# Two outlook-attention layers on one core: when the zeros of layer 0's weight tables are written

## The chip, the cores and the metric

The kernel runs on one core of a Trainium2 chip. TensorE (PE) multiplies matrices; VectorE (DVE), ScalarE (ACT) and GpSimd (POOL) work on elements; SyncE (SP) does no arithmetic here and issues most of the transfers (DMAs), each engine in its own program order. All transfers share 16 DMA engines. The metric is the device time of the whole program in microseconds, the median of several runs.

## The reference

Two layers follow each other on an image batch `x` of 8 × 56 × 56 × 384 numbers (float32), each as `x = x + layer(groupnorm(x))`. In layer 0 every pixel makes, for 12 heads, a 9 × 9 softmax from its own channels and uses it to mix the values of its 3 × 3 neighbourhood; the nine results are added back at the nine neighbours:

```
v    = einsum('bhwc,oc->bhwo', x, Wv);  vp = pad(v)
attn = softmax((x @ Wa.T).reshape(b, n, heads, 9, 9) * d ** -0.5, axis=-1)
out  = einsum('bnhpq,bnqhd->bnphd', attn, patches(vp))
y    = sum over p of out[:, :, :, p], shifted to neighbour p
return y @ Wo.T
```

Layer 1 is the same idea with 6 heads, 9 weights a pixel and no adding back. Before each layer the mean and variance of 32 groups of channels are taken per image.

## The kernel before

**Tiling.** Two images make a pair: `IMG * H` = 112 lines on the partitions. Four pairs follow each other, and within a pair the 56 columns of the image are the steps of layer 0's main loop, so a step is one column of 112 pixels. Of every eight columns seven are computed; the eighth rides in the 16 spare partitions of the seven.

**A step.** `attend` makes three score products (`bank<-wa_t`) and one value product (`bank<-wv_t`) on PE; DVE takes the maximum and subtracts it, ACT takes the exponential. Between the products other work is put in a fixed order: `stats_chunk` transposes a third of a block of the next pair's input (`pt<-xr`, four matmuls) for its group norm and keeps it in HBM (`xT`), `normalise` divides the softmax of the column before, `presum` and `fold` (four columns behind) add up the weights that meet in one pixel, and `keep_v` writes the values to a table `vtab0` in HBM through a tile `v` of two buffers.

**The weight tables.** `fold` leaves a column's weights in one of four buffers `wts` and SP writes them to a table in HBM (`ztab<-wts`, two DMAs for each patch the column belongs to). There are two tables in layer 0, `ztab0[0]` and `ztab0[1]`; patches of seven columns use them in turn. A table has 112 lines of 41 KB between margins of two and three lines. Of each of the 11 slots in a line only five of eleven rows are written by `fold`; the rest, and the margins, must be zero. The first column of the second table is written in step 9. From step 12 on `fetch_z` reads a patch of a table back (`z<-ztab`), and `contract` multiplies it by the values (`pc<-z,vp`).

**The zeros.** `fill` (line 215) writes zeros from one tile to any place of a table by one DMA on SP. `clear_weights` fills one table by seven of them: two margins, the head of each line (110 KB), two fills between the slots (1213 KB each) and two single rows. The second of the fills between reaches over the end of a line into the head of the next, so its issue waits until the fill of the heads has landed. Table 0 is filled by `clear_first` before the first step, behind the keeping of pair 0's transposed input, the zeros of `vtab0` and two fills for the first two slots of table 0. Table 1 is filled in step 3, from a list `clears` that `upkeep` works off at the end of each step.

**What sets the order.** Every engine's order is the program's (`keep_in_program_order`). In `upkeep`, the list of clears comes ahead of `stats_load`, the load of the next block of the next pair (`xr<-in_x`, 672 KB). The load that `upkeep` issues in step 3 is first used by the transposes of step 6. Transfers put into `later` (the `last` rows, residuals, results) go out at the end of a step, after `upkeep`. Every DMA of SP also waits until an earlier one with the same completion semaphore has landed; there are eight of these, taken in turn.

Of the kernel before, what the change touches and what calls it, by code (L numbers as in the profile page):

```python
# [15 lines left out]
def two_outlook_layers(  # L16
# [38 lines left out]
    R = IMG * H  # L55
    MARGIN = 2
# [16 lines left out]
    E0 = 2 * K - 1  # L73
# [8 lines left out]
    PY0, NPY0, SX0, SY0 = 7, 8, PX + 4, 11  # L82
    ROW0 = HEADS0 * PX
# [9 lines left out]
    EP0, FIRST0 = 11, 3  # L93
    EP1, FIRST1 = 11, 4
    SLOT0, SLOT1 = EP0 * ROW0, EP1 * ROW1
    LINE0, LINE1 = SX0 * SLOT0 + ROW0, SX1 * SLOT1 + ROW1
# [22 lines left out]
    ztab0 = [dram.tile([RT + 1, LINE0], F32, name=f"ztab0_{n}") for n in range(NTAB0)]  # L119
# [89 lines left out]
    def fill(table, first, dims, width):  # L209

        src = zeros[: dims[0][1], :width]
        if len(dims) > 1:
            src = src.unsqueeze(1).to_broadcast([dims[0][1], dims[1][1], width])
        tc.keep_in_program_order(
            nc.sync.dma_start(bass.AP(table.tensor, table.offset + first, [*dims, [1, width]]), src)
        )

    def clear_v(table, sx, pad):

        line = sx * C  # L220
        part = line // 12
        fill(table, 0, [[(R + GAP) * line, NPX + 1], [part, 12 * GAP]], part)
        fill(table, GAP * line, [[line, R], [C, pad]], C)
        fill(
            table, ((NPX - 1) * (R + GAP) + GAP) * line + (sx - pad) * C,
            [[line, R], [C, pad]], C,
        )

    def clear_weights(table, line, part, sx, slot, row, first, e, ep):
        fill(table, 0, [[part, MARGIN * line // part]], part)  # L230
        fill(table, (MARGIN + R) * line, [[part, (MARGIN + 1) * line // part]], part)
        top = MARGIN * line
        fill(table, top, [[line, R]], first * row)
        for n in range(2):
            between = top + (first + e) * row + n * (ep - e) * row // 2
            fill(table, between, [[line, R], [slot, sx]], (ep - e) * row // 2)

        fill(table, top + first * row, [[slot, sx]], row)
        fill(table, top + (R - 1) * line + (first + e - 1) * row, [[slot, sx]], row)

    def clear_first():

        clear_v(vtab0, SX0, 2)
        for n in range(2):
            first = MARGIN * LINE0 + FIRST0 * ROW0 + n * SLOT0
            fill(ztab0[0], first, [[LINE0, R], [E0 * ROW0 // 2, 2]], E0 * ROW0 // 2)
        clear_weights(ztab0[0], LINE0, 366, SX0, SLOT0, ROW0, FIRST0, E0, EP0)

    def clears():

        yield 3, lambda: clear_weights(
            ztab0[1], LINE0, 366, SX0, SLOT0, ROW0, FIRST0, E0, EP0
        )
        yield (NPAIR - 1) * W + 4, lambda: clear_v(vtab1, SX1, 1)
        for n, t in enumerate(ztab1):
            yield (NPAIR - 1) * W + 10 + 8 * n, lambda t=t: clear_weights(
                t, LINE1, 350, SX1, SLOT1, ROW1, FIRST1, K, EP1
            )
# [12 lines left out]
    def sort_columns(t, by, i, engine):  # L271
        engine(
            t[:, i].rearrange("k (j p) -> k j p", j=NCH), by[:, i].rearrange("k (p j) -> k j p", j=NCH)
        )

    def norm_params(st, name, params, key):

        mv = stat.tile([P, IMG, 2], F32, tag="mv", name=f"mv_{name}")

        def over_groups(src, what):  # L280
            pg = ps.tile([P, IMG], F32, tag="t", name=f"p{what}_{name}")
            matmul(pg, gmat, src, start=True, stop=True)
            g = stat.tile([P, IMG], F32, tag=what, name=f"{what}_{name}")
            vector.tensor_copy(g, pg)
            return g

        for b in range(IMG):
            vector.bn_aggr(mv[:, b, :], st[:, b].rearrange("p i n s -> p (i n) s"))
        yield
        mean = over_groups(mv[:, :, 0], "gmean")  # L290

        part = stat.tile([P, IMG], F32, tag="part", name=f"part_{name}")
        vector.tensor_sub(part, mv[:, :, 0], mean)
        vector.tensor_mul(part, part, part)
        vector.tensor_add(part, part, mv[:, :, 1])
        yield
        var = over_groups(part, "gvar")
        std = stat.tile([P, IMG], F32, tag="std", name=f"std_{name}")
        scalar.activation(std, var, AF.Sqrt, bias=eps_t)
        scale = const.tile([P, IMG], F32, name=f"scale_{name}")  # L300
        vector.reciprocal(scale, std)
        bias = const.tile([P, IMG], F32, name=f"bias_{name}")
        vector.scalar_tensor_tensor(bias, mean, -1.0, scale, ALU.mult, ALU.mult)
        params[key] = scale, bias
        yield
# [120 lines left out]
    def layer0(late, pools):  # L426
# [12 lines left out]
        def stats_load(pair, blk, queue, xr):  # L439
            xrs[pair, blk] = xr  # L440
            queue.dma_start(xr, xf[pair * R : (pair + 1) * R, blk * XB : (blk + 1) * XB, :])
# [3 lines left out]
        def xr_tile(pair, blk):  # L445
            t = xr_bufs[blk % 2]
            return t[:R].rearrange("r (m c) -> r m c", m=XB)
# [130 lines left out]
        def load(g):  # L578
            pair, blk = divmod(g, NBLK)
            xins[g] = io.tile([P, XB, NCH, R], F32, tag="xin", name=f"xin_{g}", bufs=1)  # L580
            sync.dma_start(
                xins[g], xTs[pair][:, blk * XB : (blk + 1) * XB]
            )

        def normed(g, parts, both=False):

            scale, bias = params[g // NBLK]
            xin, to = xins[g], xns[g // 2 % 2]
            n = XB - g % 2
            for shared, b in parts:  # L590
                rows = slice(b * H, (b + 1) * H)
                if shared:
                    if not g % 2:
                        continue
                    dst = to[:, :, :, R + b * PART : R + (b + 1) * PART]
                    src = xin[:, n, :, rows].rearrange("p i (j y) -> p i j y", j=NTILE)
                else:
                    dst = to[:, :, g % 2 * XB : g % 2 * XB + n, rows]
                    src = xin[:, :n, :, rows].rearrange("p m i r -> p i m r")
                if both and b:  # L600
                    vector.tensor_scalar(
                        dst, src, scale[:, b : b + 1], bias[:, b : b + 1], ALU.mult, ALU.add
                    )
                else:
                    scalar.activation(
                        dst, src, AF.Identity, bias=bias[:, b : b + 1], scale=scale[:, b : b + 1]
                    )
# [275 lines left out]

        making = {}
        clearing = list(clears())

        def upkeep(step):

            pair, c = divmod(step, W)
            if pair == 0:  # L890
                if c == 1:
                    gpsimd.memset(wts, 0.0)
                if c == 3:
                    by = z_flat[0][:, : NCH * C].rearrange("p (i n) -> p i n", i=NCH)
                    sync.dma_start(by, wo0.rearrange("(i p) n -> p i n", p=P))
                if 5 <= c < 5 + NCH:
                    by = z_flat[0][:, : NCH * C].rearrange("p (i n) -> p i n", i=NCH)
                    sort_columns(wo_t, by, c - 5, vector.tensor_copy)
            while clearing and clearing[0][0] <= step:
                clearing.pop(0)[1]()  # L900
            if pair + 1 < NPAIR:
                blk, i = divmod(c - 3, NCH)
                if i == 0 and blk < NBLK - 1 and pair + c:
                    stats_load(pair + 1, blk + 1, sync, xr_tile(pair + 1, blk + 1))
                if NBLK * NCH + 3 <= c < NBLK * NCH + 6:
                    if c == NBLK * NCH + 3:
                        making["0"] = norm_params(stats.pop(pair + 1), f"0_{pair + 1}", params, pair + 1)
                    next(making["0"])
            g, j = divmod(step + 2 * XB, XB)
            if j < NCH and g < NPAIR * NBLK:  # L910
                normed(g, SHARED if j == IMG else WHOLE[j : j + 1])
            if step < IMG:
                normed(1, WHOLE[step : step + 1])
            if j == NCH - 1 and 2 < g + 1 < NPAIR * NBLK and g > 2:
                load(g + 1)
# [413 lines left out]
```

## Time and profile before

| what | value |
|---|---|
| time, median of 3 runs | 3188.24 us (3183.09 to 3190.77) |
| the profiled execution: its time | 3187.7 us |
| its span | 3185.5 us |
| mean granted TensorE clock | 0.989 |
| busy: PE, DVE, POOL, ACT | 96%, 65%, 52%, 32% |
| DMA queue of SP and ACT (q1) | 711.31 MB, 73.7% of 16 engines |
| DMA queue of POOL (q0) | 116.90 MB, 11.8% |
| zeros of tables 0 and 1 | 14 DMAs, issued between 70.5 and 103.8 us |

The profile is of one execution, in microseconds from its first instruction. A row of the timeline gives start, length, engine, line, operation, what it writes and reads, how many were merged, and in brackets how long the engine was idle before it and what ended that. "SPq" rows are DMA issues of SP: their length is the time the issue held the queue, and the transfer lands later. Until about 57 us the kernel takes the statistics of pair 0; then step 0 begins, and a step takes 6 to 9 us. Columns are numbered like the steps; on PE a column's end is its value product `bank<-wv_t`.

### The profile page before, as it was taken

The page shows a single profiled execution, that of the slowest core. Times are in us where ns is not written, and L with a number is a line of the kernel's source. Part 1 is how long each engine was busy: PE and PEld are TensorE (multiplying, and loading weights), DVE is VectorE, ACT ScalarE, POOL GpSimd, SP SyncE. Part 2 cuts the span into 40 slices and gives each one's busy share as a digit, 9 for nine tenths or more (in the row PEclk, how much of TensorE's full clock was granted, in tenths as well). Part 3 has the DMA queues.
Part 4 walks back from the last instruction along what each step waited for, and adds up shares of the span by engine and source line. Part 5 has one row for each costly group of instructions (what it writes and reads, how often), then busy time and mean ns, then how long its engine had stood idle before and what let it go on. Part 6 is the DMA issues. An engine that isn't in the chain of part 4 may idle for free. (4 is left out here: it accounts for less than half of the span.)

```text
span 3185.5 us, 72855 instructions
## 1 busy us (share of the span) xinstructions
PE 3065.3 (96%) x27640; PEld 2093.4 (66%) x27640; DVE 2084.8 (65%) x4942; ACT 1005.2 (32%) x2422; POOL 1654.2 (52%) x2759
## 2 busy tenths in 40 slices
PE   6899999999999999999999999989999999999997
PEld 5667766777776677776776666645666565656655
DVE  5777777777777777777777777635454555555454
ACT  4333333343333334333333333222222222222221
POOL 2765665655556565656566566544334344434431
PEclk8999999999999999999999999999999999999999
DMA  9799987899997899988888987889899988989897
GB/s 303 225 306 319 307 273 260 300 296 300 325 311 235 275 305 303 314 280 286 280 250 262 309 275 247 286 279 242 219 230 246 234 235 228 251 222 241 233 236 154
DMA packets 619842, 850.86 MB, mean 267 GB/s; under 512 B 264926, under 2 KB 496562, under 8 KB 611170
## 3 DMA queue, kind: packets, MB, share of 16 engines
q1 hardware_dynamic: 522322, 711.31, 73.7%
q0 software_dynamic: 63824, 116.90, 11.8%
q10 hardware_dynamic: 33344, 17.98, 2.1%
q8 instruction: 218, 3.57, 0.5%
q14 instruction: 134, 1.10, 0.1%
HBM read 514.86 MB, written 322.17 MB: 263 GB/s over the span
## 5 line engine op out<-in xcount | busy, mean ns | idle before, releaser
L128 PE MATMUL bank<-wa_t,xn 128*128 128x288 f32 x3528 | 967.8, 411 | 15.7 <-ACT xn L143 10.3
L128 PE MATMUL po<-yT,wo_t 128*128 128x448 f32 (+1 forms) x2304 | 817.0, 497 | 26.5 <-DVE x1t L143 19.4
L143 POOL TENSOR_TENSOR at<-at,d 128x972 f32<-128x972 f32 x196 | 441.2, 2251 | 714.8 <-DVE d L143 387.7
L128 PEld LDWEIGHTS bank<-wa_t,xn 128*128 128x128 f32 x3528 | 647.7, 191 | 226.2 <-issue 17.6
L128 PEld LDWEIGHTS po<-yT,wo_t 128*128 128x128 f32 x2304 | 433.6, 191 | 328.7 <-issue 195.8
L143 ACT ACTIVATE at<-at 128x972 f32<-128x972 f32 (+1 forms) x228 | 215.3, 944 | 997.1 <-DVE at L143 992.3
L1104 POOL DMA_DIRECT2D at<-lgt x392 | 204.8, 526 | 591.9 <-DVE lgt L143 580.8
L143 DVE TENSOR_REDUCE mx<-bank 128x36 f32<-128x324 f32 x588 | 284.8, 484 | 311.2 <-PE bank L128 309.3
L128 PE MATMUL bank<-wc_t,xn 128*128 128x438 f32 x1176 | 478.8, 543 | 5.1 <-DMA wc_t<-in_wv 5.1
L143 ACT COPY yT<-pc 128x294 f32<-128x294 f32 (+2 forms) x512 | 198.5, 405 | 804.9 <-PE pc L128 803.5
L128 PE MATMUL bank<-wv_t,xn 128*128 128x384 f32 x1176 | 414.5, 489 | 0.0
L128 PEld LDWEIGHTS pc<-z,vp 121*32 121x32 f32 (+1 forms) x17664 | 337.6, 120 | 111.9 <-issue 69.2
L128 PE MATMUL pc<-z,vp 121*32 121x49 f32 (+1 forms) x17664 | 374.2, 218 | 23.2 <-DMA z<-ztab 7.9
L128 PEld LDWEIGHTS bank<-wc_t,xn 128*128 128x128 f32 x1176 | 215.6, 191 | 180.9 <-issue 167.8
L143 DVE TENSOR_TENSOR at<-bank,mx 128x324 f32<-128x324 f32 x588 | 291.5, 496 | 31.0
L128 PEld LDWEIGHTS bank<-wv_t,xn 128*128 128x128 f32 x1176 | 220.8, 190 | 132.0 <-issue 9.3
L143 POOL DMA_DIRECT2D vtab<-v x476 | 289.5, 612 | 12.2 <-issue 6.8
L143 POOL TENSOR_TENSOR pre<-at,at 112x108 f32<-112x108 f32 (+1 forms) x440 | 236.5, 538 | 85.0 <-DMA at<-at 36.2
L143 DVE TENSOR_TENSOR lgt<-bank,ba_t 128x54 f32<-128x54 f32 x196 | 42.0, 214 | 308.7 <-PE bank L128 308.7
L333 POOL DMA_DIRECT2D vtab<-v x392 | 211.6, 544 | 16.0 <-issue 7.8
L143 DVE SCALAR_TENSOR_TENSOR wide<-po,bo_t,wide 128x448 f32<-128x448 f32 (+1 forms) x156 | 97.5, 625 | 167.4 <-PE po L128 167.3
L143 ACT ACTIVATE wts<-pre,inside 112x48 f32<-112x48 f32 (+4 forms) x672 | 179.3, 358 | 78.1 <-DMA ztab<-wts 66.2
(111 smaller groups left out, 2816.9 us busy)
## 6 DMA issues: line engine op xcount, KB each, us to landing
z<-ztab SPq DMA_DIRECT2D x64, 2352.0 KB
vp<-vtab SPq DMA_DIRECT2D x64, 1536.0 KB
vp<-vtab SPq DMA_DIRECT2D x64, 945.0 KB
xres<-xT SPq DMA_DIRECT2D x32, 1176.0 KB
ztab<-wts SPq DMA_DIRECT2D x336, 110.2 KB
vtab<-v POOLq DMA_DIRECT2D x108, 336.0 KB, 6.6
xin<-xT SPq DMA_DIRECT2D x52, 672.0 KB
xr<-in_x SPq DMA_DIRECT2D x50, 672.0 KB
```

Of the source, the lines that this page charges most:

```text
L128: tc.keep_in_program_order(nc.tensor.matmul(*args, **kwargs))
L143: return lambda *args, **kwargs: tc.keep_in_program_order(op(*args, **kwargs))
L333: queue.dma_start(bass.AP(table.tensor, table.offset + first, [*([line * step, count] for step, count in rows_of or ((1, rows),)), *([[(R ...
L1104: nc.gpsimd.dma_start(at_of(g_of)[row : row + n, m_of].rearrange("r k h -> r (k h)"), lg[lo : lo + n])
```

## The change

`clear_weights` is divided into `clear_lines`, which fills a range of lines (heads and the two fills between the slots), and `clear_rest` (margins and the two single rows). For layer 0's tables the lines are filled in four pieces of 28, one at the end of a step: table 0 in steps 1 to 4 and its rest in step 5, table 1 in steps 7 to 10 and its rest in step 11. `clear_first` keeps the zeros of `vtab0` and the two fills of the first slots. The work on the list moves behind `stats_load` in `upkeep`. In layer 1 the tables are still filled whole, with the rest now ahead of the lines. The bytes are the same; SP issues 32 DMAs for the two tables where it issued 14, and 1800 rows in all against 1782. The order of the instructions on PE, DVE, ACT and POOL does not change.

```diff
-    def clear_weights(table, line, part, sx, slot, row, first, e, ep):
+    def clear_lines(table, line, sx, slot, row, first, e, ep, lo, hi):
+        top = (MARGIN + lo) * line
+        fill(table, top, [[line, hi - lo]], first * row)
+        for n in range(2):
+            between = top + (first + e) * row + n * (ep - e) * row // 2
+            fill(table, between, [[line, hi - lo], [slot, sx]], (ep - e) * row // 2)
+
+    def clear_rest(table, line, part, sx, slot, row, first, e):
         fill(table, 0, [[part, MARGIN * line // part]], part)
         fill(table, (MARGIN + R) * line, [[part, (MARGIN + 1) * line // part]], part)
         top = MARGIN * line
-        fill(table, top, [[line, R]], first * row)
-        for n in range(2):
-            between = top + (first + e) * row + n * (ep - e) * row // 2
-            fill(table, between, [[line, R], [slot, sx]], (ep - e) * row // 2)
-
         fill(table, top + first * row, [[slot, sx]], row)
         fill(table, top + (R - 1) * line + (first + e - 1) * row, [[slot, sx]], row)
+
+    def clear_weights(table, line, part, sx, slot, row, first, e, ep):
+        clear_rest(table, line, part, sx, slot, row, first, e)
+        clear_lines(table, line, sx, slot, row, first, e, ep, 0, R)
...
-        clear_weights(ztab0[0], LINE0, 366, SX0, SLOT0, ROW0, FIRST0, E0, EP0)
 
     def clears():
 
-        yield 3, lambda: clear_weights(
-            ztab0[1], LINE0, 366, SX0, SLOT0, ROW0, FIRST0, E0, EP0
-        )
+        for step, table in ((1, ztab0[0]), (7, ztab0[1])):
+            for n in range(4):
+                yield step + n, lambda t=table, n=n: clear_lines(
+                    t, LINE0, SX0, SLOT0, ROW0, FIRST0, E0, EP0, n * R // 4, (n + 1) * R // 4
+                )
+            yield step + 4, lambda t=table: clear_rest(t, LINE0, 366, SX0, SLOT0, ROW0, FIRST0, E0)
...
-            while clearing and clearing[0][0] <= step:
-                clearing.pop(0)[1]()
             if pair + 1 < NPAIR:
                 blk, i = divmod(c - 3, NCH)
                 if i == 0 and blk < NBLK - 1 and pair + c:
                     stats_load(pair + 1, blk + 1, sync, xr_tile(pair + 1, blk + 1))
...
+            while clearing and clearing[0][0] <= step:
+                clearing.pop(0)[1]()
```

## The prediction, made before the changed kernel was run

> **What bounds the kernel now.** I read the page first, then a cut of the trace into stretches of about one column each, then the timelines of SP, PE and DVE where a stretch is poor, then the waits. The page's busy shares and its slices:
>
> ```profile
> PE 3065.3 (96%) x27640; PEld 2093.4 (66%) x27640; DVE 2084.8 (65%) x4942; ACT 1005.2 (32%) x2422; POOL 1654.2 (52%) x2759
> PE   6899999999999999999999999989999999999997
> PEclk8999999999999999999999999999999999999999
> ```
>
> PE bounds the run: 120.2 us of the 3185.5 us span are all that it idles, and over a third of this lies in the first 300 us. What a change near the start can win is PE's idle time there; afterwards PE is full, so a saving stays. The cut by stretches (columns: PE, PEld, DVE, ACT, POOL busy with counts, PE clock, DMA share, GB/s):
>
> ```profile
> 78.00:87.00 9.00, 7.90 (x32) 5.24 (x31) 7.18 (x17) 1.93 (x3) 8.92 (x13) 1.00 0.93 271
> 95.50:103.00 7.50, 7.50 (x35) 5.62 (x34) 5.29 (x13) 3.02 (x6) 4.68 (x9) 1.00 1.00 299
> 103.00:111.50 8.50, 1.55 (x7) 0.88 (x5) 5.91 (x12) 2.08 (x3) 6.68 (x10) 0.87 0.93 292
> 111.50:119.00 7.50, 7.47 (x25) 5.77 (x26) 3.11 (x8) 1.27 (x4) 4.97 (x11) 0.69 0.52 148
> 128.00:135.00 7.00, 7.00 (x33) 5.34 (x32) 4.77 (x11) 3.62 (x8) 4.84 (x11) 1.00 0.28 81
> 135.00:143.00 8.00, 7.63 (x34) 5.53 (x33) 7.29 (x18) 3.52 (x8) 6.18 (x10) 1.00 0.64 169
> 143.00:151.00 8.00, 7.54 (x33) 5.38 (x32) 7.29 (x20) 2.69 (x7) 6.48 (x10) 1.00 0.70 203
> 151.00:159.00 8.00, 7.86 (x35) 5.46 (x33) 7.40 (x18) 2.70 (x7) 5.48 (x9) 1.00 0.76 239
> ```
>
> One stretch stands out: from 103 to 111.5 PE works 1.55 of 8.5 us, and in the next its clock is 0.69. In 135 to 159 DVE is as full as PE (21.98 of 24 us). The timeline of PE there:
>
> ```profile
> 83.50 1.72 PE L128 MATMUL bank<-wa_t,xn 128*128 128x288 f32 x6 [1.10 <-ACT v L143]
> 92.26 1.72 PE L128 MATMUL bank<-wa_t,xn 128*128 128x288 f32 x6 [1.33 <-ACT v L143]
> 111.53 0.99 PE L131 MATMUL pt<-ident,xr 112*128 112x112 f32 x4 [6.98 <-DMA xr<-in_x]
> 112.32 3.11 PE L128 MATMUL bank<-wa_t,xn 128*128 128x288 f32 x6
> ```
>
> PE waits 6.98 us for the second input block of pair 1, and works the next product at a lower clock (3.11 us; the others take 1.72). SP's timeline says why the block is late:
>
> ```profile
> 64.56 23.14 SPq L215 DMA_DIRECT2D ztab<-zeros  x9
> 91.63 12.20 SPq L215 DMA_DIRECT2D ztab<-zeros  x7
> 104.35 1.09 SPq L143 DMA_DIRECT2D xr<-in_x  x1
> ```
>
> SP spends 35 us on the fills of the two tables; the load is issued behind both. The timeline of DVE and two answers of SP's waits (58 to 104 us, then 119 to 159) give the rows for the costs:
>
> ```profile
> 115.47 0.50 DVE L143 TENSOR_REDUCE mx<-bank 128x36 f32<-128x324 f32 x1 [6.26 <-PE bank L128]
> ```
> ```profile
> SPq L215 <- DMA ztab<-zeros: 7.8, 2, 4.6
> ```
> ```profile
> SPq L143 <- DVE wts L143: 23.8, 5, 8.9
> ```
>
> **The change, part by part.**
>
> (a) Column 6's wait goes. PE, DVE, ACT and POOL keep their order; SP alone changes. Ahead of the load now stand the two band fills (SP is through them at 70.5), the pieces of columns 1 and 2 (six fills), two writes to `last` and Wo's load. A piece's third fill overlaps its first, so SP waits until that has landed; the next piece's first waits for the third. That is three landing waits ahead of the load. The two such waits of before took 3.2 and 4.6 us (7.8 less 4.6), so 9.6 to 13.8 us. The nine issues: before, nine fills took 23.14 less 3.2, or 2.2 us each, and seven 12.20 less 4.6, or 1.1 each: 9.9 to 19.8 us. So the load goes out between 70.5 + 19.5 = 90 and 70.5 + 33.6 = 104 us, against 104.35. I take about 92: the fills are a quarter as large, and the slow issues were those behind the older writes. Landing took at most 7.2 us (104.35 to 111.53): about 99. PE is ready for the block at 104.55 (111.53 less 6.98), so the wait disappears.
>
> Its worth: PE's distance from column 5's to column 6's value product is 117.53 less 100.99, 16.5 us; the later distances are 7.2 and 7.8 (126.43, 133.60, 141.40), so by PE alone 9.0 us come back, clock included. DVE says less: its gap is 6.26 us, and behind it DVE works nearly without a break. In the 16 us from 103 to 119 it was busy 9.02; at the 0.916 of 135 to 159 that takes 9.85 us, 6.2 saved. Both ends stay; I take 6.3, as DVE is the fuller engine in the columns after.
>
> (b) The waits of 1.10 and 1.33 us in columns 3 and 4 are for `v` buffers whose writes to `vtab` land late among table 0's zeros. The first lies before the pieces can thin the traffic; the second should go. 1.3 taken, 0 to 2.4 possible.
>
> (c) Table 1's 2.74 MB of zeros (110 + 2 × 1213 + 200 + 7 KB) move from 91 to 104 us into columns 7 to 11. At the 299 GB/s of 95.5 to 103 that is 9.2 us of DMA time. Free in 128 to 159: 0.72 × 7 + 0.36 × 8 + 0.30 × 8 + 0.24 × 8 = 12.2 us. It fits, with 3 us to spare, so its cover is thin; next would come late `v` landings, as in (b). I charge one of these, 1.2; bounds 0 and 9.2.
>
> (d) SP issues 32 fills in place of 14, and the 4 pieces of table 1 each add one landing wait. Queued behind are that column's xT and `last` writes, the next column's `ztab` writes, in column 10 the load of xin, in column 11 vp's fetch. Those who wait for them are ACT and DVE for a `wts` buffer (two or more columns later), POOL for `last`, ACT for xin. SP stands free 23.8 us in five waits, 4.8 a column; a piece needs 3.2 to 4.6 plus three issues of 0.4: 4.4 to 5.8. Cost 0 taken, 4 × 1.0 the upper end. Table 0's margins, filled in column 5, wait for the weight writes just issued (one more landing, 3.2 to 4.6) and column 6's weight write for them; 0 taken, since that write is next awaited two columns on. Layer 1's fills change only their order within a table: 0.
>
> A rule speaks against (d): in the Trainium skill, DMA: Bandwidth & Descriptors, Rules for kernel authors, small transfers are to be coalesced, and Anatomy of one DMA there gives each about 2.0 us that do not shrink with size. By it 18 more would cost an estimated 36 us, were each on the path. The rows above show landing waits even longer than that, but on a queue with idle time.
>
> The same page (Why a DMA increments its semaphore by 16 and not by 1) says that a DMA uses the largest number of engines up to 16 that divides its outermost dimension, 14 for a 28-line piece. By it (c) would be an estimated 10.5 us. No row of the run before has a 28-line transfer.
>
> Sum: −6.3 − 1.3 + 1.2 = −6.4 us. The profiled execution took 3187.7 us, 0.5 below the median of the runs shown (3188.24): 3181.3 on its own time, 3181.8 on the median; I say 3181.5. From 159 us on DMA is next to bound (0.95 and more to 200 us, with fetches of `vp` and `z`); those move up with the columns and get no new bytes, the pieces being out by column 11.
>
> **Rivals.**
> - PE's reckoning holds, and both `v` waits go: 9.0 + 2.4 = 11.4, 3176.8 us. For it: the slow clock after the wait costs 1.4 us on one product alone. Against: DVE at 92% afterwards.
> - The load is no earlier: at the slow end of (a) it goes out at 104. Nothing is won: 3188. For it: fills took 2.2 us each to issue. Against: those stood behind the 9.4 MB of pair 0's transposed input, which the DMAs have written by about 70 us (376 GB/s from 65 to 72 us, 125 from 72 to 78).
> - Slower: SP becomes the bound of columns 7 to 10. Without pieces it is busy 3.2 us of 7.8 there (issues of 1.80, 0.49, 0.59 and 0.35 from 144.5 on). A landing wait above 3.4 us (7.8 − 3.2 − 1.2) begins to make it late; at 5.0 us four columns have eaten the 6.4; at 7.4 us, about what the late `xr` took to land (7.2), they cost 16 and the run ends at 3198, 0.3% above before. Against: DMA is at 0.28 to 0.76 there, `v` landing in 3.3 to 5.1 us between 128 and 150, and `wts` gives two columns of room.
>
> **How the numbers follow.** Forecast 0.42, PE's reckoning 0.30, load no earlier 0.15, slower 0.13. A measurement tells about 0.3% (9.6 us) from no change, so the forecast and the unmoved load are "same" save for the upper edge of the first, PE's reckoning "faster": 0.33, 0.53, 0.14. The range goes from PE's reckoning less half the spread of the three runs (3176.8 − 3.8 = 3173) to no gain plus the same (3188.2 + 3.8 = 3192); the slow case and a larger gain are left out.
>
> **What would show it.** After: SP issues the second `xr` near 92 us, PE's 6.98 us wait on `xr` and the clock of 0.69 are gone, column 6's value product comes about 6 to 9 us earlier, DVE has no gap over 1 us there; in columns 7 to 11 the DMA share rises to about 0.9 with no new PE wait over 1.5 us; every later landmark is earlier by the same amount. Wrong if SP waits for a fill's landing over 5 us a piece, if a new wait for `xr`, `xin` or `wts` opens before column 16, or if PE's idle time from 160 to 210 us grows.

## The result and the profile after

| | before | after |
|---|---|---|
| median of 6 runs | 3187.59 us (3183.09 to 3197.83) | 3203.02 us (3199.51 to 3206.35) |
| ratio to before, 95% interval | | 1.0044 (1.0028 to 1.0060) |
| span of the profiled execution | 3185.5 us | 3199.7 us |
| mean granted clock | 0.989 | 0.986 |

The change makes the kernel 0.44% slower, 15 us by the medians and 14.2 by the spans. The forecast was 3181.5 us, and the range ended at 3192: both missed. The page of after, its busy shares and its first rows of slices:

```profile
PE 3071.8 (96%) x27640; PEld 2097.9 (66%) x27640; DVE 2081.8 (65%) x4942; ACT 1005.8 (31%) x2422; POOL 1651.9 (52%) x2759
...
PE   6879999999999999999999999989999999999998
...
PEclk8989999999999999999999999989999999999999
```

PE did the same 27640 matmuls. Its third slice (160 to 240 us) has fallen from 9 to 7, and the clock there from 9 to 8: the loss lies early, and where it lies can be read from one landmark per column, the start of its value product `bank<-wv_t` (us, from the timelines of PE):

| column | 5 | 6 | 8 | 12 | 13 | 14 | 16 | 17 | 18 |
|---|---|---|---|---|---|---|---|---|---|
| before | 100.99 | 117.53 | 126.43 | 157.28 | 165.33 | 173.07 | 188.32 | 197.04 | 209.63 |
| after | 101.59 | 108.77 | 120.17 | 152.30 | 161.61 | 173.29 | 196.96 | 205.68 | 223.80 |
| difference | +0.6 | −8.8 | −6.3 | −5.0 | −3.7 | +0.2 | +8.6 | +8.6 | +14.2 |

Column 6's gain is there; from column 12 on it is lost, and by column 18 the whole 14.2 us of the end are made. After 230 us the two profiles stay 14 to 18 us apart. The cut of after by the stretches shown of before (PE, PEld, DVE, ACT, POOL busy with counts, clock, DMA share, GB/s), with one for columns 13 to 18 added:

```profile
95.50:103.00 7.50, 7.09 (x33) 5.28 (x32) 6.54 (x14) 3.12 (x6) 5.97 (x10) 1.00 0.64 186
103.00:111.50 8.50, 8.50 (x41) 6.41 (x40) 8.17 (x19) 3.04 (x6) 6.68 (x10) 1.00 0.80 210
111.50:119.00 7.50, 4.56 (x26) 3.68 (x25) 6.64 (x17) 4.25 (x10) 7.42 (x12) 1.00 0.58 149
...
135.00:143.00 8.00, 7.31 (x33) 5.41 (x32) 6.48 (x18) 2.79 (x7) 7.92 (x14) 1.00 0.91 207
143.00:151.00 8.00, 6.77 (x30) 4.55 (x29) 7.40 (x18) 2.80 (x7) 6.10 (x10) 1.00 0.65 180
151.00:159.00 8.00, 6.12 (x25) 4.37 (x25) 5.24 (x16) 1.85 (x5) 5.77 (x9) 1.00 0.71 160
160.00:225.00 65.00, 46.67 (x533) 35.14 (x533) 32.18 (x87) 20.30 (x47) 31.45 (x50) 0.82 0.88 289
```

The hole at 103 to 111.5 us is gone (PE 8.50 of 8.5 us, 1.55 before, clock 1.00). But at 151 to 159 PE is busy 6.12 us (7.86 before) and DVE 5.24 (7.40), with the DMA share at 0.71: neither a full engine nor a full DMA explains that. In the last stretch PE had, before:

```profile
160.00:225.00 65.00, 58.73 (x604) 43.08 (x603) 46.39 (x121) 25.33 (x57) 42.78 (x69) 0.97 0.90 304
```

PE's idle time there is 18.3 us in place of 6.3, at a clock of 0.82 in place of 0.97. SP's timeline of after from column 7's piece to the first fetch of `z` (start, time held, what it issued; a row merges the DMAs of one kind and the waits between them):

```profile
90.35 0.92 SPq L143 DMA_DIRECT2D xr<-in_x  x1
...
122.46 7.21 SPq L215 DMA_DIRECT2D ztab<-zeros  x3
130.21 2.67 SPq L143 DMA_DIRECT2D ztab<-wts  x2
133.10 4.83 SPq L215 DMA_DIRECT2D ztab<-zeros  x3
138.03 2.83 SPq L143 DMA_DIRECT2D ztab<-wts  x4
141.43 7.44 SPq L215 DMA_DIRECT2D ztab<-zeros  x3
149.67 2.92 SPq L143 DMA_DIRECT2D ztab<-wts  x4
152.64 3.57 SPq L215 DMA_DIRECT2D ztab<-zeros  x3
158.56 5.26 SPq L143 DMA_DIRECT2D ztab<-wts  x4
...
177.72 0.39 SPq L143 DMA_DIRECT2D z<-ztab  x1
```

From 122.46 to 163.82 us SP has hardly a gap. Before, the last three groups of four weight writes ahead of the first fetch of `z` went out at 144.53, 152.20 and 160.18 us, and the fetch at 164.47; here 149.67, 158.56, 169.59 and 177.72. So SP's work is 13 us late by the fetch, though PE was still ahead at column 13. SP's waits in after, from 59 to 225 us (in total, times, longest, us):

```profile
SPq L215 <- DMA ztab<-zeros: 32.9, 12, 6.3
SPq L143 <- DMA z<-ztab: 7.6, 1, 7.6
SPq L215 <- DMA ztab<-wts: 6.1, 2, 3.5
...
SPq L143 <- DVE wts L143: 5.2, 3, 4.5
```

Before, the same window had:

```profile
SPq L143 <- DVE wts L143: 48.3, 12, 8.9
SPq L215 <- DMA ztab<-zeros: 7.8, 2, 4.6
SPq L143 <- DMA z<-ztab: 6.9, 1, 6.9
```

The fourth line of after is SP's slack: time in which it waited for work from DVE. It was 48.3 us and is 5.2. Landing waits of zeros, 7.8 us in 2, are now 32.9 in 12, and two more (6.1 us) are the margins' fills waiting behind weight writes just issued. Five of the twelve, 17.4 us, lie between 119 and 160 us. That SP's lateness reaches the engines is in the waits of ACT and DVE, 111 to 225 us, of after:

```profile
ACT wts L143 <- DMA ztab<-wts: 30.2, 6, 8.1
...
DVE wts L143 <- DMA ztab<-wts: 19.1, 4, 8.8
```

Before, these were one wait of 7.0 and one of 4.4 us. A `wts` buffer comes free when its write has landed, and the write now goes out late.

### The profile page after: what moved, and what is told of

Same layout as the page of the kernel before. It is cut to its first block, busy times and chain, and to the rows that moved or that the text cites. A ratio compares the mean times of both kernels' runs of the same rounds, so it can differ in the third digit from the quotient of the medians.

```text
span 3199.7 us, 72872 instructions
## 1 busy us (share of the span) xinstructions
PE 3071.8 (96%) x27640; PEld 2097.9 (66%) x27640; DVE 2081.8 (65%) x4942; ACT 1005.8 (31%) x2422; POOL 1651.9 (52%) x2759
## 3 DMA queue, kind: packets, MB, share of 16 engines
q8 instruction: 218, 3.57, 0.5%
## 5 line engine op out<-in xcount | busy, mean ns | idle before, releaser
L128 PE MATMUL bank<-wa_t,xn 128*128 128x288 f32 x3528 | 970.8, 412 | 18.9 <-ACT xn L143 10.4
```

The costliest lines, as they stand in the source:

```text
L128: tc.keep_in_program_order(nc.tensor.matmul(*args, **kwargs))
```

## The experiments

Theory S: the loss is SP's landing waits. A fill that overlaps an earlier one holds SP until that has landed, and with it the column's other transfers. Rivals: D, the zeros themselves, moved into columns 7 to 10, crowd the DMAs there; N, the number of DMAs (32 in place of 14) is the cost; R, the new order alone, the load ahead of the zeros, brings the next transfers into collision and gains nothing. All ratios are to the kernel before on the same chip, with 95% intervals.

**The load ahead of the zeros, and nothing else.** The kernel before, with the work on the list moved behind the load:

```diff
-            while clearing and clearing[0][0] <= step:
-                clearing.pop(0)[1]()
             if pair + 1 < NPAIR:
...
+            while clearing and clearing[0][0] <= step:
+                clearing.pop(0)[1]()
```

> The kernel before with one part of the change alone: the list of clears is worked off behind the column's loads, the fills are whole as before. Both theories: PE's wait of 7 us on the block in column 6 goes, column 6 ends 6 to 9 us earlier and the time is 3178 to 3183 us. If what is won there is given back later whatever the zeros do, 3186 to 3189.

Measured 0.9986 (0.9975 to 0.9997). Of 3187.59 us that is 3183, the upper end of the first expectation. SP in this kernel:

```profile
93.04 1.10 SPq L143 DMA_DIRECT2D xr<-in_x  x1
94.19 13.43 SPq L215 DMA_DIRECT2D ztab<-zeros  x7
```

The load leaves at 93.04 us, nearly where the pieces bring it (90.35), and column 6's value product starts 6.2 us earlier than before (column 5's is 3.2 later, 1.4 of it since column 0). R is out as the source of a loss: the interval lies below 1. From column 5 to column 8 it gains 5.3 us (20.19 in place of 25.44). But what stays against before is less than the 6.2: −2.1 at column 8, −1.3 at columns 16 and 17, +0.7 at 18.

**Pieces that don't overlap.** After, with a piece's first fill cut so that it ends where the second of the fills between has written (that one runs over the line's end into the next line's head):

```diff
+    def clear_apart(table, line, sx, slot, row, first, e, ep, lo, hi):
+        top, over = (MARGIN + lo) * line, (first - 1) * row
+        if lo == 0:
+            fill(table, top, [[line, 1]], over)
+        fill(table, top + over, [[line, hi - lo]], row)
+        for n in range(2):
+            between = top + (first + e) * row + n * (ep - e) * row // 2
+            fill(table, between, [[line, hi - lo], [slot, sx]], (ep - e) * row // 2)
...
-                yield step + n, lambda t=table, n=n: clear_lines(
+                yield step + n, lambda t=table, n=n: clear_apart(
```

> The changed kernel, with the same bytes in the same columns, but the fills of a piece no longer overlap (the head of a line is filled only where the fill of the line before does not reach it), so SP need not wait for a landing inside a piece or between pieces; the waits of the two margins stay. Theory S (SP's landing waits, 32.9 us against 7.8 before, make SP late in columns 7 to 11): those waits fall under 5 us and the time to 3179 to 3186 us. Theory D (the zeros' bytes beside the columns' own transfers delay everything): the time stays within 4 us of the changed kernel, 3199 to 3207.

Measured 1.0013 (1.0004 to 1.0022): 0.31 of the 0.44% is gone with the waits inside and between the pieces, at the same columns, with two DMAs more and nearly the same bytes (only the doubled ones are gone, 0.07 of 2.74 MB a table). That speaks for S and against D and N, but of 3187.59 us the ratio is 3192, short of the 3179 to 3186 that S had expected. SP's slack, and what is left of its waits for the tables' fills:

```profile
SPq L143 <- DVE wts L143: 17.3, 8, 5.5
SPq L215 <- DMA ztab<-wts: 7.9, 2, 4.0
```

The second line is the margins of each table, filled one column after its last piece, behind weight writes that they overlap.

**Margins early as well.** The same, with the margins and single rows in the column of the second piece:

```diff
-            yield step + 4, lambda t=table: clear_rest(t, LINE0, 366, SX0, SLOT0, ROW0, FIRST0, E0)
+                if n == 1:
+                    yield step + 1, lambda t=table: clear_rest(t, LINE0, 366, SX0, SLOT0, ROW0, FIRST0, E0)
```

> pieces_apart with the margins and single rows of a table filled one column after its first piece, before any weight is written to it, so that no fill waits for a landing any more (pieces_apart kept 7.9 us of SP waiting for weight writes). The bytes stay in columns 1 to 4 and 7 to 10. If the rest of the loss is those two waits: 3 to 8 us below pieces_apart, ratio to before 0.998 to 1.0005. If it is the bytes and issues themselves in columns 7 to 10: within 3 us of pieces_apart, ratio 1.0005 to 1.0022.

Measured 0.9994 (0.9985 to 1.0003). With only one landing wait of 0.9 us left on zeros, SP issues 34 DMAs for the two tables where it issued 14 and the kernel is not slower than before. N and D together are what lies between this and 0.9986: 0.08%, with overlapping intervals, so neither can be told from nothing. The two margin waits were worth 0.19%, about 6 us, by intervals that just don't overlap.

**Waits put in alone.** The load-first kernel, plus in each of columns 7 to 10 two fills of the same 28 line heads (28 KB each), the second over the first:

```diff
+        def twice(n):
+            for _ in range(2):
+                fill(ztab0[1], (MARGIN + n * R // 4) * LINE0, [[LINE0, R // 4]], FIRST0 * ROW0)
+
+        for n in range(4):
+            yield 7 + n, lambda n=n: twice(n)
```

> load_first, and in each of columns 7 to 10 a piece's heads (28 KB) are filled twice, the second fill waiting for the landing of the first: a landing wait without the bytes. It writes zeros over zeros. Theory S: each wait holds SP 3 to 7 us, and the time is 8 to 20 us above load_first. Theory D: within 3 us of load_first.

Measured 0.9999 (0.9991 to 1.0008), against 0.9986 without them; the intervals overlap slightly, and the difference (0.13%, some 4 us) lies between the two expectations, nearer D's. SP's waits:

```profile
SPq L215 <- DMA ztab<-zeros: 25.4, 7, 6.1
SPq L143 <- DVE wts L143: 14.6, 5, 7.3
```

Almost no bytes, and 17.2 us more of landing waits than in the load-first kernel (8.2 us in 2), 15.5 of them the four waits inside the pairs: SP's slack falls from 41.0 to 14.6 us. So waits use up the slack; that they alone take time is likely but not shown, and what they take is far less than their sum and less than the change took. A reason may be that SP has not waited as long in the columns before these four; this was not tested.

**Table 0 in pieces, table 1 whole.** After, with table 1 filled at once in column 3, behind the load:

```diff
-        for step, table in ((1, ztab0[0]), (7, ztab0[1])):
+        for step, table in ((1, ztab0[0]),):
             for n in range(4):
+                if step + n == 4:
+                    yield 3, lambda: clear_weights(
+                        ztab0[1], LINE0, 366, SX0, SLOT0, ROW0, FIRST0, E0, EP0
+                    )
                 yield step + n, lambda t=table, n=n: clear_lines(
```

> The changed kernel with table 0 in pieces in columns 1 to 5 as there, but table 1 filled whole in column 3, behind the load. If the pieces of table 1 alone cost (both theories place the loss in columns 7 to 18): 3178 to 3185. If table 0's pieces cost as well, since SP is late from column 1 on: 3188 to 3200.

Measured 1.0021 (1.0010 to 1.0031): half of the loss is there without any piece of table 1. Here column 6 comes 10.3 us earlier and column 9 is 6.7 late. PE says why:

```profile
135.01 0.99 PE L131 MATMUL pt<-ident,xr 112*128 112x112 f32 x4 [5.29 <-DMA xr<-in_x]
```

Table 1's seven fills come between table 0's third and fourth piece (the third and the seven fill SP's time from 90.92 to 104.14 us); the fourth is issued at 110.44 and the margins at 126.36 us, where after had them at 102.98 and 113.60. The next load of `xr` leaves behind all that at 129.60 us (117.86 before): the old wait has moved on by one block. So this kernel does not measure table 0's pieces alone.

**Load first, whole fills that don't overlap.** The load-first kernel, with each table filled by eight fills that don't overlap:

```diff
...
+        fill(table, (MARGIN + R) * line, [[part, (MARGIN + 1) * line // part]], part)
+        fill(table, 0, [[part, MARGIN * line // part]], part)
+        fill(table, top, [[line, 1]], over)
+        fill(table, top + over, [[line, R]], row)
+        between(0)
...
+        between(1)
```

> load_first with the fills of a table whole but not overlapping, and put in an order in which hardly any waits for another to land (load_first kept 8.2 us of such waits, in columns 0 to 5). If SP's lateness in the first columns still costs: 2 to 5 us below load_first, ratio to before 0.997 to 0.998. If SP has caught up by column 6 whatever it waits before: as load_first, 0.998 to 0.9995.

Measured 0.9987 (0.9977 to 0.9997), the same as with the overlaps (0.9986). SP's landing waits on zeros are 2.3 us here, 8.2 there: 5.9 us of them in the first columns, where SP has slack behind them, cost nothing that shows.

**The late fetch, made short.** Every kernel so far that still leads before at column 14 (by 1.9 to 6.5 us) gives up most or all of it by column 18, where DMA is full. There SP also waits for the second fetch of `z` to land before it may write table 0's weights again (6.9 to 8.1 us in each of them). The two `z` fetches of pair 0's first patch were cut to one of their eight parts in two kernels, before and after. The result is then wrong, and two `memset`s of POOL fill what is not fetched:

```diff
-    gpsimd.memset(zs[1][:, NZ0:], 0.0)
+    gpsimd.memset(zs[0][:, 4260:NZ0], 0.0)
+    gpsimd.memset(zs[1][:, 4032:], 0.0)
...
-                sync, zs[b], ztab0[(pair * NPX + px) % NTAB0], LINE0, SLOT0, ROW0, 0, GROUPS0,
-                b, PY0, NPY0,
+                sync, zs[b][:, :1] if not pair and not px else zs[b], ztab0[(pair * NPX + px) % NTAB0], LINE0, SLOT0, ROW0, 0, GROUPS0,
+                b, PY0, 1 if not pair and not px else NPY0,
```

> The kernel before with the first two fetches of weights (pair 0, first patch) cut to one of their eight parts, 0.3 instead of 2.4 MB each; the contraction of that patch then works on other numbers, in the same time. It is the base for z_short_after. The DMAs have 4.1 MB less to bring between 160 and 200 us; 4 to 12 us below before.

> The changed kernel with the same cut. If the loss is made where SP, late from columns 7 to 11, issues these fetches late and then waits for the second to land before it may write table 0 again (columns 12 to 18, DMA full): the loss goes with the fetches, and the time is 2 to 8 us below z_short_before. If the landing waits cost by themselves, through weight buffers that come free late in columns 8 to 12: still 8 to 16 us above z_short_before.

Measured 0.9984 (0.9974 to 0.9995) and 0.9996 (0.9985 to 1.0008). With the cut the change costs 0.12%, some 4 us, which these intervals don't tell from nothing, where it cost 0.44% without; that is between the two expectations. Yet the waits upstream are all there:

```profile
SPq L215 <- DMA ztab<-zeros: 33.3, 12, 5.7
```

So SP's waits are where the loss begins, and the stretch of columns 14 to 18, where DMA has no room, is where most of their lateness becomes time. With the fetches cut, the value product of column 17 comes within 0.2 us of that of the kernel before with the same cut (8.6 us late without the cut).

**The same cut, with the pieces that don't wait.**

> The pieces that don't overlap, margins filled a column early (0.9994 as they stood), and of pair 0's first z fetch only an eighth of the lines is fetched (the rest of that z is wrong data of the same size; the time of all else is kept). If the 6.5 us won at column 6 are lost only behind that fetch, they should now stand beside the cut's own gain (0.9984 for the kernel before with the same cut): 0.996 to 0.9975. If they are lost to the full DMA of columns 12 to 18 whatever the one fetch does, the ratio stays at 0.9978 to 0.999.

Measured 0.9976 (0.9967 to 0.9985), between the two expectations: it doesn't decide. In its profile the lead over before stays at 6.5 to 7.2 us from column 18 to 1287 us (0.8 of it at column 18 is the cut's own), with PE busy 36.05 of 40 us from 160 to 200 against 30.27 without the cut, so in the first pair the lead is lost behind those fetches. In that one execution nearly all of it goes again between 1287 and 1500 us (0.7 left), in a later pair; single executions of one kernel lie 10 to 17 us apart, so nothing is read from that.

**Loads of `xr` a column earlier.** In the kernel of pieces that don't wait, PE's longest wait in the full stretch was 8.89 us for `xr` at 202 us, whose load leaves after the second `z` fetch. Two kernels issue each block's load a column earlier, one with those pieces, one on the load-first kernel:

```diff
-                if i == 0 and blk < NBLK - 1 and pair + c:
-                    stats_load(pair + 1, blk + 1, sync, xr_tile(pair + 1, blk + 1))
+                if c == 0 and pair:
+                    stats_load(pair + 1, 0, sync, xr_tile(pair + 1, 0))
+                if i == NCH - 1 and blk < NBLK - 2:
+                    stats_load(pair + 1, blk + 2, sync, xr_tile(pair + 1, blk + 2))
```

> The same pieces, whole z fetches, and the loads of xr for each block issued a column earlier, so that they stand ahead of the late z fetch on SP. If the wait of PE on xr (8.9 us at 202 us) is where the lead of column 6 goes, 0.9970 to 0.9982. If VectorE's wait of 11.5 us on the weight lines, behind the same fetch, is the one that ends last, 0.999 to 1.000, no change.

> Zeros whole, only moved behind the loads (0.9986 as it stood), with the loads of xr a column earlier. If xr's lateness is what costs there too, 0.996 to 0.998; if the full DMA of columns 12 to 18 sets the pace, 0.998 to 0.9995; and if the earlier loads of xr only push the zeros back, 0.999 to 1.000.

Measured 1.0041 (1.0029 to 1.0054) and 1.0018 (1.0008 to 1.0028): slower than without the edit by 0.47 and 0.32%, outside every range expected. My reason was wrong: `xr` was only the wait that ended last. In the first of the two, PE and DVE:

```profile
203.81 2.19 PE L128 MATMUL pc<-z,vp 121*32 121x49 f32 x96 [5.73 <-DMA z<-ztab]
```
```profile
204.55 0.16 DVE L143 MEMSET wts<- 112x120 f32 x1 [12.17 <-DMA ztab<-wts]
```

against, without the edit,

```profile
202.44 0.99 PE L131 MATMUL pt<-ident,xr 112*128 112x112 f32 x4 [8.89 <-DMA xr<-in_x]
```
```profile
201.14 0.16 DVE L143 MEMSET wts<- 112x120 f32 x1 [11.54 <-DMA ztab<-wts]
```

The 672 KB now go ahead of the second `z` fetch, which left at 188.12 us in place of 182.72, and PE waits for `z` instead; DVE's wait for a `wts` buffer, behind that fetch, lasts about as long and ends 3.4 us later. The edit also moves the loads of the later pairs, and part of its cost is made there; that part was not taken apart.

The ladder, then: as changed 1.0044; no waits in and between the pieces 1.0013; none behind the margins either 0.9994; the load moved alone 0.9986.

## Why the prediction was wrong

- **(a), right.** The load left at 90.35 us, where about 92 was taken. The three landing waits ahead of it were shorter than the rows used (6.5 us in all, 9.6 to 13.8 reckoned). PE's and DVE's waits of 6.98 and 6.26 us went, and from column 5 to column 8 PE needed 18.58 us in place of 25.44: 6.9 us, between DVE's reckoning (6.3) and PE's (9.0), nearer the first, as chosen. (DVE was not quite "as full as PE" there: 21.98 us of 24, PE 23.03.) Every kernel with the load ahead of the zeros has column 6 earlier than before, by 6.2 to 10.4 us, but for the load-first one with `xr` a column earlier (2.2).
- **(b), wrong and small.** The first `v` wait stayed (1.56 us in after), the second went from column 4 and one of 0.41 us came in column 5; a gain of 1.3 us is not to be seen: column 5 comes 0.6 us late, just as column 0 does.
- **(c), right as to room.** The zeros fitted: the DMA share from 128 to 159 us is 0.65 to 0.91. The late `v` charged with 1.2 us did not come: ACT's waits for `vtab<-v` from 58 to 225 us are 4.5 us in 2, 6.0 in 3 before.
- **(d), the step that failed: "Cost 0 taken".** The size of a piece was near the reckoning: four pieces held SP for 7.21, 4.83, 7.44 and 3.57 us, 5.8 in the mean, the upper end of "4.4 to 5.8". But that end is above the 4.8 us a column that SP had free, and I took 0 because the lower end was below. In place of 0 the waits in and between the pieces of both tables were worth 0.31% of the time, some 10 us (1.0044 to 1.0013), and the margins' two waits, "0 taken" for table 0's and without a price for table 1's, 0.19%. Two things were left out. The pieces of table 0 wait in the same way (14.2 us in six waits by 104 us, 7.8 in two before); what these cost was not separated. And the weight writes held SP longer (four of them 2.83 to 5.26 us, 1.76 to 1.80 before); but they do so too with the pieces that don't wait (2.65 to 4.65 us), which keep their lead to column 17, so this alone is not the loss.
- **"Afterwards PE is full, so a saving stays"; the later transfers "move up with the columns": the failing close of the sum.** From 160 to 200 us the DMA share is 0.94 to 1.01 in before, after, the load-first kernel and the two with pieces that don't overlap. Even where SP doesn't wait for zeros and the lead is 7.1 us at column 17, column 18 is 1.3 late: by these shares, and by the waits of PE (8.89 us for `xr`) and DVE (11.54 for `ztab<-wts`) there, the stretch is paced by transfers, and a lead in PE does not shorten them. The shortened fetches show that those of the first patch are part of that; what else paces the stretch is open. In after it also got new bytes: the rest of table 1's zeros, meant for column 11, left at 166.56 us. In before, 120 to 160 had a share of 0.68, 160 to 200 of 1.00; in the pieces that don't wait:

```profile
120.00:160.00 40.00, 38.97 (x166) 28.11 (x165) 34.77 (x85) 15.56 (x36) 29.59 (x47) 1.00 0.90 251
160.00:200.00 40.00, 30.27 (x305) 22.23 (x304) 22.32 (x57) 11.78 (x26) 26.52 (x43) 0.91 0.99 333
```

  PE loses 9.7 us of 40 in the second, 4.1 before. So 6.4 was the wrong gain even with (d) at 0: it would be a ratio of 0.9980, and the pieces that don't wait measured 0.9994 (0.9985 to 1.0003). What these runs show can be had is the 0.14% of the moved load, 4.5 us, by an interval of 0.03 to 0.25%.
- **The slower rival** was the right mechanism, with 0.13 of the chance and a price that was too low. It counted four columns of table 1, decided from 3.4 us a wait, and set 3198 at 7.4. In its columns the five waits averaged 3.5 us (17.4 / 5) and the longest was 6.3, by which it would have cost next to nothing; the run ended at 3203. The bound is not the single wait but the slack used up over twelve of them, and the stretch in which lateness turns into time.
- The signs named for a wrong prediction came as written: a landing wait above 5 us, `wts` waits before column 16, and more idle PE time from 160 us on.

The rule of the Trainium skill weighed there (DMA: Bandwidth & Descriptors, Rules for kernel authors: coalesce small transfers) pointed the right way, but not for the reason it gives: 34 fills with next to no landing waits measured 0.9994, so no cost per transfer showed (and the 2.0 us of that page's Anatomy of one DMA are fitted on transfers issued by GpSimd, while SP issues these). What bore on the case is another sentence of that section: a wait on a semaphore takes place on the issuing sequencer, before dispatch. The 32.9 us in twelve such waits on SP are that, measured.

## What to carry to other kernels

Before a large transfer is cut into pieces, look whether the pieces overlap each other or anything just written: each overlap is a landing wait on the queue that issues, and the queue's slack (its waits for work of other engines, summed over the stretch) is what it is paid from. Make the pieces disjoint, or move only the order: here disjoint pieces with the margins early took the loss away but gained nothing that shows (0.9994), and the moved loop alone gave 0.9986, where the whole change gave 1.0044. And a gain on PE ahead of a stretch where DMA is full is to be counted only after asking what that stretch waits for.

## What the runs showed of the hardware

- A small write is no quick one to wait for: in after, with the DMA share at 0.65 to 0.91, the waits for fills of 28 and 303 KB lasted up to 6.3 us, and in the kernel with the pairs, with the share at 0.37 to 0.85, the waits for a 28 KB fill lasted 2.4 to 5.5.
- The same issue can hold its queue longer: four weight writes held SP 1.76 us at 160.18 us of before, and 5.26 at 158.56 us of after (0.30 to 0.42 us each, against up to 1.90). SP's waits in that stretch of after put 3.1 us of it down to instructions of ACT and DVE (`xt`, `d`, `v`, `mx`), none of which writes what is sent; what held it was not tested.
- A load issued earlier can cost: two kernels whose only edit was `xr` a column earlier lost 0.32 and 0.47%.
